# Two matmul groups moved ahead of a third, and a weight pass with another schedule, in a one-core decoder layer

## The chip, the cores and the metric

The kernel runs on one core of one Trainium2 chip. The metric is the device time of one execution in microseconds (us). Five engines take part, each with an instruction queue of its own that it works through in order: TensorE (PE, matmuls; its weight loads are PEld), VectorE (DVE), ScalarE (ACT), GpSimd (POOL) and SyncE (SP). SP and POOL also issue most transfers, each on a DMA queue of its own; both queues share 16 DMA engines. An instruction that waits for a semaphore holds up everything behind it on its engine.

## The reference

A decoder layer on x (2 x 512 tokens, 1024 features) is computed in float32, in three parts:

```
x = x + attn(layernorm(x))     # mamba2 block, then an MLP
x = x + fake_quant(layernorm(x)) @ fake_quant(ctx)
x = x + ffn(layernorm(x))
```

Two stages matter here. The MLP at the end of the first part is

```
mlp = silu(h2 @ gate_w.T) * (h2 @ up_w.T) @ down_w.T     # 1024 -> 3584 -> 1024
```

and the last part needs a mean over its own weights before it can begin:

```
def _binary_diff_weight(w, base):
    d = w - base
    coeff = jnp.mean(jnp.abs(d))
    return base + coeff * jnp.sign(d)     # for w1, w2 and w3
```

sign(d) and the sum of |d| depend on weights alone, so they can be computed at any time before the last part.

## The kernel before

**Order of the stages.** mamba2 takes the first 460 us or so, then the MLP's gates run to about 1110 us, its down product to about 1442, with the quantised product beside it and shortly behind, and from about 1446 us the gates and then the down product of the last part, which use the same functions.

**The gates** (`gates`) work in NG = 14 groups of 256 hidden columns. In a group, gate and up are each a product of a 1024 x 256 weight with the activations, split by a Strassen-Winograd scheme into seven products of blocks, 1 to 7. Products 1 and 2 go into one tile O12. In groups 0 and 1 they are plain matmuls: `first_two` makes four steps, each four matmuls into a PSUM bank (tile ma, line 355) and a copy to O12 by ScalarE (line 361). From group 2 they are a second level of the scheme (`second_level`, tiles mm2a to mm13d, lines 876 to 901). Products 6 and 7 are always a second level (tiles mn0a to mn13d). Products 5, 4 and 3 are plain (`one`, line 1027, tiles m0c, m0d); product 3 accumulates onto a bank of product 5 or 4 that DVE has read before (`onto`).

The order on TensorE is written out by hand and kept by chains (`on_pe`, `on_act`, `on_dve`): each instruction of a chain is issued after the one before it. In group 0 it is products 4 and 5, then mn0, then m0c onto m0c (product 3); then group 1 begins with ma. What closes a group, `finished`, `last_product` and `put` (the last sums, the product h3, the sums of mh and their store mhd), runs in the next group's beginning, through the list `late`.

**In `second_level`** four banks a, b, c, d are filled in the order a, b, c, d, b, a, c. The last matmul group adds onto c, and must wait until DVE has read c for the sum C22 (lines 199 and 202 are the helpers `add` and `sub` that make all these sums). `summed` runs between DVE's first sum (u2) and the second (u3): in mm it calls `last_product`, in mn `summed67`.

**The weight pass** (`Diffs`) is the side work in the MLP's gates: 34 steps, each for one weight group of the last part. A step subtracts the base from the weight (DVE, tile sw, 128 x 2048), takes Sign (ScalarE, line 1458, into the base's own tile, smean_w) and Abs with its sum (line 1459), stores the signs (POOL's queue, line 1460), and calls `load` for a later step (two transfers of 1 MB on POOL's queue, line 1449). POOL's transfers are kept in program order. Weight and base have two slots each (pool raw, tags raw and base). `gates` calls a step as `side` at three points of a group: in `summed67`, after the three products of `product`, and in `last_product`. In group order these are called C, A and B below: A ends group i, B stands in the mm and C in the mn of group i + 1.

After the gates, `down` reads the stored blocks back on SP's queue (line 1281) into places that include the pool raw's; in its first calls of `work` it also finds coeff from the sums (`find_coeff`, line 1498).

Of the kernel before, what the change touches and what calls it, by code (L numbers as in the profile page):

```python
# [10 lines left out]
F32 = mybir.dt.float32  # L11
# [6 lines left out]
P = 128  # L18
NB = 2
L = 512  # L20
D = 1024
KC = D // P
# [3 lines left out]
GW = 256  # L26
NG = INTER // GW
# [11 lines left out]
def decoder(ctx, tc, a, out):  # L39
# [266 lines left out]
    last = {}  # L306
# [9 lines left out]
    def on_act(fn):  # L316
        return ordered(act_last, fn)
# [10 lines left out]
    def last_on(engine):  # L328
        return next(ins for ins in reversed(traced) if ins.engine == engine)
# [11 lines left out]

        return {x: g.enter_context(tiles_waited(name=f"{name}{x}", bufs=counts.get(x, POOLS[x]), **kw)) for x in names}

    def first_two(name, act, pl, i, gw, uw, banks):

        O = pl["o12" if "o12" in pl else "o1"].tile([P, 2, 2, L], F32, tag="o", name=f"{name}o12_{i}")
        ps = []

        def step(p, x, w):
            if not p:  # L350
                ps.append(bank(banks[x], f"{name}a{x}_{i}"))

            def product():
                for k in range(4):
                    nc.tensor.matmul(  # L355
                        ps[x], w[:, 4 * p + k, :P], act[0][:, 4 * p + k, :],
                        start=not p and k == 0, stop=k == 3, skip_group_check=p > 0,
                    )

            on_pe(product)  # L360
            on_act(lambda: nc.scalar.copy(O[:, p, x, :], ps[x]))  # L361

        return O, [lambda p=p, x=x, w=w: step(p, x, w) for p in range(2) for x, w in enumerate((gw, uw))]

# [61 lines left out]
    with ExitStack() as m:  # L426
# [10 lines left out]
        pl = {  # L437
            "p1": proj.enter_context(tiles_waited(name="wp1", bufs=2)),
            "tmp": proj.enter_context(tiles_waited(name="wtmp", bufs=3)),
        }  # L440
# [296 lines left out]
        o = m.enter_context(tiles_waited(name="wout", bufs=1))  # L737
# [129 lines left out]

    def second_level(name, banks, p1, A, B, O, copied=lambda: None, summed=lambda: None, early=False, between=lambda: None):


        ps = {x: bank(k, f"{name}{x}", (P, 2, Q)) for x, k in zip("abcd", banks)}

        def mm(x, i, onto=False):
            for q in range(2):
                for k in range(2):
                    nc.tensor.matmul(
                        ps[x][:, q, :], A[i][:, q, k, :], B[i][q][:, k, :] if isinstance(B[i], tuple) else B[i][:, q, k, :],
                        start=not onto and q == 0 and k == 0, stop=k == 1, skip_group_check=onto or q > 0,
                    )

        c11, u2, u3, c22 = (O[:, :, x, c : c + Q] for x in (0, 1) for c in (0, Q))
        on_pe(lambda: mm("a", 1))
        on_act(lambda: nc.scalar.copy(p1, ps["a"]))
        copied()
        on_pe(lambda: mm("b", 6))
        on_dve(lambda: add(u2, p1, ps["b"]))
        summed()
        on_pe(lambda: mm("c", 5))
        if early:
            on_pe(lambda: mm("a", 2, True))  # L890
            on_act(lambda: nc.scalar.copy(c11, ps["a"]))
            on_pe(lambda: mm("b", 7, True))
            on_pe(lambda: mm("d", 4))
        else:
            on_pe(lambda: mm("d", 4))
            on_pe(lambda: mm("b", 7, True))
        on_dve(lambda: add(u3, p1, ps["b"]))
        on_dve(lambda: add(c22, u3, ps["c"]))
        if not early:
            on_pe(lambda: mm("a", 2, True))  # L900
            on_act(lambda: nc.scalar.copy(c11, ps["a"]))
        between()
        on_dve(lambda: add(u3, u3, ps["d"]))
        on_pe(lambda: mm("c", 3, True))
        on_dve(lambda: add(u2, u2, ps["c"]))
# [3 lines left out]
    def gates(name, act, acts, g, pl, weights, down_weight, begun, ex, side, third=()):  # L909
# [14 lines left out]
        with g:  # L924
# [73 lines left out]
            coming = [weights(0, None), weights(1, None)]  # L998
            w2, stored = [down_weight(0, None)], None
            A, A67 = left(0, *coming[0])  # L1000
            for i in range(NG):
                last = i == NG - 1
# [37 lines left out]
                elif i < 2:  # L1040
                    O12, steps = first_two(name, act, pl, i, *coming[0], X)
# [22 lines left out]
                if i == 0:  # L1064
                    c, d = (one("c", 4), one("d", 5)) if third else (one("c", 5), one("d", 4))
                elif third and i == 1:
                    c = one("d", 4)
# [5 lines left out]
                O67 = pl["o67"].tile([P, 2, 2, L], F32, tag="o", name=f"{name}o67_{i}")  # L1073

                def summed67(i=i, O12=O12):
# [8 lines left out]
                    if third:  # L1084
# [3 lines left out]
                            A54 = third_left(i, *coming[0])  # L1088
                        on_act(lambda: nc.scalar.activation(O12[:, 1, 0], O12[:, 1, 0], AF.Silu))

                second_level(f"{name}n{i}", Y, p1, A67, B67, O67, summed=summed67)
                on_dve(lambda: add(O67[:, 0], O12[:, 0], O67[:, 0]))

# [5 lines left out]
                turn = on_dve(lambda: add(O67[:, 1], O67[:, 0], O67[:, 1]))  # L1099
                h = pl["hp"].tile([P, 7, L], F32, tag="h", name=f"{name}h{i}")  # L1100
                C12, C22, C21 = O67[:, 0], O12[:, 0], O67[:, 1]
                if more:
                    c = one("c", 3)
                elif third:
                    e = one("c" if i else "e", 3)
                    if i:
                        d = one("e", 5)
                else:
                    if i:
                        c = one("c", 5)  # L1110
                    onto(C22, C21, c)
                    if i:
                        d = one("d", 4)
                    blocks21 = onto(C21, C21, d)
                    one("c", 3, True)
                coming.pop(0)
                if not last:
                    with tc.issue_after(turn):
                        steps = [], []
# [5 lines left out]
                if i == 1:  # L1125
                    b = act[0].rearrange("p (q k) l -> p q k l", q=2)
# [37 lines left out]
                    onto(O67[:, 0], O67[:, 0], c, on_dve)  # L1164
                    on_act(lambda: nc.scalar.activation(O67[:, 0, 0], O67[:, 0, 0], AF.Silu))

                def last_product(O67=O67, h=h, last=last):
                    if not last:
                        side(on_dve)
                    on_dve(lambda: nc.vector.tensor_tensor(h[:, 3, :], O67[:, 0, 0], O67[:, 0, 1], ALU.mult))  # L1170

# [34 lines left out]
                if third and last:  # L1206

                    def last_stores(i=i, h=h):
                        nc.sync.dma_start(dram[0][i][:, 1:3, :], h[0][:, 1:3, :])
                        hidden_blocks(h[0])  # L1210
                        nc.sync.dma_start(dram[0][i][:, 3:, :], h[0][:, 3:, :])

                    hl = []
                    def first_slot(finished_third=finished_third, hl=hl, i=i):
                        nc.sync.dma_start(hl[0][:, 0, :], dram[0][i][:, 0, :])
                        finished_third()

                    rest.extend([first_slot, lambda hl=hl: last_products(h=hl[0]), lambda hl=hl: last_stores(h=hl), hl.append])
                elif third:
                    late.extend([finished_third, last_products, put])  # L1220
                else:
                    for slot, o in ((0, O12[:, 1]), (2, C22), (1, C21)):
                        product(slot, o)
                    if not last:
                        with tc.issue_after(blocks21):
                            side(lambda fn: fn())
                    late.extend([finished, last_product, put])
# [185 lines left out]
    pl = {**mpl, **open_pools(g, "m", ("raw",))}  # L1413
# [20 lines left out]
    class Diffs:  # L1434
# [16 lines left out]
        def step(self, dve):  # L1451
            if self.n == len(self.todo):
                return
            i, j = self.todo[self.n]
            w, b = self.raw.pop(self.n)
            dve(lambda: sub(w, w, b))
            sg = b.bitcast(BF16)[:, : KC * GW]
            on_act(lambda: nc.scalar.activation(sg, w, AF.Sign))  # L1458
            on_act(lambda: nc.scalar.activation(w, w, AF.Abs, accum_out=sums[:, j, 2 * i : 2 * i + 1]))  # L1459
            ordered(self.pool_last, lambda: nc.gpsimd.dma_start(signs[j][i], sg))  # L1460
            self.load(self.n + 2)
            self.n += 1

    diffs = Diffs()
# [28 lines left out]
    def find_coeff():  # L1493
        nc.vector.tensor_reduce(tot, sums, AX.X, ALU.add)
        ones = xp.tile([P, P], F32, name="ones")
        nc.gpsimd.memset(ones, 1.0)
        ps = psx.tile([P, 512], F32, tag="x", name="cps2")
        nc.tensor.matmul(ps[:, 0:3], ones, tot, start=True, stop=True)
        nc.vector.tensor_scalar(coeff, ps[:, 0:3], 1.0 / (INTER * D), None, ALU.mult)
# [102 lines left out]
    steps = [0]  # L1602

    def work():
        steps[0] += 1
        if steps[0] == 4:
            find_coeff()
        if steps[0] == 10:
            contexts[0].load()
        if steps[0] in (12, 13):  # L1610
            contexts[0].column(steps[0] - 12)
        for _ in range(2):
            if pending:
                pending.pop(0)()
# [6 lines left out]
    pl = open_pools(held, "f", ("o12", "o67"))  # L1621
# [42 lines left out]
    third = [more[:, k].rearrange("p (q b c) -> p q b c", q=2, b=2) for k in range(3)]  # L1664
# [81 lines left out]
```

## Time and profile before

| | us |
|---|---|
| time, median of 3 runs | 2394.27 |
| lowest and highest run | 2389.66 to 2397.71 |
| span of the profiled execution (its own time) | 2391.7 |
| TensorE busy in it | 2337.4 |
| VectorE busy | 1744.0 |
| ScalarE busy | 620.2 |
| weight pass, first and last subtraction start | 497.5 and 994.0 |
| TensorE busy from 500 to 550 us, of 50 | 41.21 |
| TensorE busy from 569 to 1036 us, of 467 | 465.30 |

The span runs from the first to the last instruction of one execution. Lines of the profile are read like this. A group line names the source line, engine and operation, the tile written and the tiles read (out<-in), and a count. In a listing in order of time the first two numbers are the start and the duration in us; what stands in brackets at the end is the time that the engine idled just before and what ended it. A line of waits reads "who <- for whom: us in total, times, longest". A line of transfers gives the issuing queue, the count, the KB of each and the us from issue to landing. A matmul of float32 is two records, so that x8 is a group of four.

### The profile page before, as it was taken

The page shows a single profiled execution, that of the slowest core. Times are in us where ns is not written, and L with a number is a line of the kernel's source. Part 1 is how long each engine was busy: PE and PEld are TensorE (multiplying, and loading weights), DVE is VectorE, ACT ScalarE, POOL GpSimd, SP SyncE. Part 2 cuts the span into 40 slices and gives each one's busy share as a digit, 9 for nine tenths or more (in the row PEclk, how much of TensorE's full clock was granted, in tenths as well). Part 3 has the DMA queues.
Part 4 walks back from the last instruction along what each step waited for, and adds up shares of the span by engine and source line. Part 5 has one row for each costly group of instructions (what it writes and reads, how often), then busy time and mean ns, then how long its engine had stood idle before and what let it go on. Part 6 is the DMA issues. An engine that isn't in the chain of part 4 may idle for free.

```text
span 2391.7 us, 24259 instructions
## 1 busy us (share of the span) xinstructions
PE 2337.4 (98%) x9020; PEld 1649.0 (69%) x9028; DVE 1744.0 (73%) x2537; ACT 620.2 (26%) x800; POOL 207.0 (9%) x246
## 2 busy tenths in 40 slices
PE   7999999989999999999999999999999999999999
PEld 5445444446667667667888784578787787888888
DVE  5658777577888888865655756798888888775554
ACT  3355460333243234200000325122232232100000
POOL 1124211101011011000000101000000000000000
PEclk9999999999999999999999999999999999999999
DMA  4353541668888888838755471667677576786651
GB/s 160 115 201 120 183 173 71 163 243 325 313 329 336 309 328 335 294 156 299 229 165 161 131 228 54 179 167 203 192 190 210 165 206 205 249 261 196 191 176 63
DMA packets 183925, 494.80 MB, mean 207 GB/s; under 512 B 21504, under 2 KB 125952, under 8 KB 152832
## 3 DMA queue, kind: packets, MB, share of 16 engines
q1 hardware_dynamic: 155648, 334.91, 40.2%
q0 software_dynamic: 23552, 149.96, 21.7%
q10 hardware_dynamic: 4608, 8.39, 0.9%
q8 instruction: 71, 1.16, 0.2%
q14 instruction: 46, 0.38, 0.1%
HBM read 349.52 MB, written 145.75 MB: 207 GB/s over the span
## 4 chain that ended last, share of the span: by engine, by line
PE 62%; DVE 23%; DMA 5%; issue 4%; ACT 3%; SPq 2%; POOL 1%; DVEq 0%; POOLq 0%; ACTq 0%
PE op L769 3%; DVE fo L199 2%; DVE sw L202 2%; SPq L1281 2%; DVE mpl L199 2%; DVE fy L202 2%; DVE mo L199 1%; DVE down L202 1%; DVE mpl L202 1%; ACT smean_w L1458 1%; DVE fw L199 1%; DVE acc L635 1%; PE fa L355 1%; DMA f1b<-fwd 1%; PE dps L503 1%
## 5 line engine op out<-in xcount | busy, mean ns | idle before, releaser
L1458 ACT ACTIVATE smean_w<-sw 128x2048 bf16<-128x2048 f32 x34 | 65.0, 1911 | 177.3 <-DVE sw L202 177.3
L1641 ACT ACTIVATE fw<-fpl,coeff 128x2048 f32<-128x2048 bf16 x38 | 75.9, 2000 | 33.0 <-PE f1e L1027 12.9
L1642 POOL DMA_DIRECT2D fw<-in_mean_w x42 | 36.5, 869 | 544.9 <-DVE fo L199 310.2
L202 DVE TENSOR_TENSOR sw<-sw,smean_w 128x2048 f32<-128x2048 f32 x34 | 77.6, 2284 | 3.7 <-DMA smean_w<-in_mean_w 3.7
L1459 ACT ACTIVATE sw<-sw 128x2048 f32<-128x2048 f32 x34 | 64.9, 1910 | 1.1
L199 DVE TENSOR_TENSOR fo<-fo,fo 128x1024 f32<-128x1024 f32 x50 | 61.2, 1225 | 3.8 <-ACT fw L1641 0.5
L414 POOL TENSOR_TENSOR raw<-raw,base 128x1024 f32<-128x1024 f32 x16 | 44.4, 2777 | 199.1 <-DMA base<-in_mean_w 55.9
L769 PE MATMUL op<-wout,mz 128*128 128x512 f32 x128 | 56.6, 592 | 0.0
L1460 POOL DMA_DIRECT2D sign<-smean_w x34 | 18.3, 538 | 295.4 <-ACT smean_w L1458 295.3
L769 PEld LDWEIGHTS op<-wout,mz 128*128 128x128 f32 x128 | 23.9, 190 | 27.7 <-issue 27.0
L1188 ACT ACTIVATE fo<-fo 128x512 f32<-128x512 f32 x42 | 26.2, 630 | 43.8 <-DVE fo L199 43.8
L202 DVE TENSOR_TENSOR down<-down 128x512 f32<-128x512 f32 x56 | 37.2, 682 | 0.1
L1159 ACT ACTIVATE mo<-mo 128x512 f32<-128x512 f32 x28 | 17.7, 632 | 68.9 <-DVE mo L199 68.8
L199 DVE TENSOR_TENSOR fw<-fw 128x512 f32<-128x512 f32 x52 | 34.5, 684 | 0.4
L199 DVE TENSOR_TENSOR hid<-hid,op 128x512 f32<-128x512 f32 x24 | 15.9, 683 | 24.2 <-PE op L769 24.2
L202 DVE TENSOR_TENSOR fy<-fw,fw 128x512 f32<-128x512 f32 x48 | 32.9, 686 | 0.4
L355 PE MATMUL fa<-x3T,fw 128*128 128x512 f32 x64 | 30.4, 624 | 2.1 <-ACT fo L361 2.1
L199 DVE TENSOR_TENSOR fo<-fo 128x1024 f32<-128x1024 f32 x26 | 31.8, 1221 | 0.5
L1159 ACT ACTIVATE mpl<-mpl 128x512 f32<-128x512 f32 x14 | 8.8, 630 | 89.0 <-DVE mpl L199 89.0
L202 DVE TENSOR_TENSOR mh<-mh 128x512 f32<-128x512 f32 x42 | 29.0, 689 | 0.9
L1449 POOL DMA_DIRECT2D smean_w<-in_mean_w x34 | 18.2, 534 | 126.6 <-DMA sign<-smean_w 50.4
L1560 PE MATMUL xa<-c,c1T 128*128 128x512 bf16 x122 | 28.1, 379 | 0.5 <-issue 0.2
(2514 smaller groups left out, 6011.2 us busy)
## 6 DMA issues: line engine op xcount, KB each, us to landing
fw<-in_mean_w POOLq DMA_DIRECT2D x42, 1024.0 KB, 11.5
sw<-in_w POOLq DMA_DIRECT2D x34, 1024.0 KB, 7.8
smean_w<-in_mean_w POOLq DMA_DIRECT2D x34, 1024.0 KB, 7.6
mwd<-down SPq DMA_DIRECT2D x14, 1792.0 KB, 5.7
mhd<-mh SPq DMA_DIRECT2D x13, 1792.0 KB, 10.3
fhd<-fh SPq DMA_DIRECT2D x13, 1792.0 KB, 8.1
fpl<-sign SPq DMA_DIRECT2D x38, 512.0 KB, 8.8
sign<-smean_w POOLq DMA_DIRECT2D x34, 512.0 KB, 6.0
```

What stands on the lines that cost most here:

```text
L199: return nc.vector.tensor_tensor(out_, x, y, ALU.add)
L202: return nc.vector.tensor_tensor(out_, x, y, ALU.subtract)
L355: nc.tensor.matmul(ps[x], w[:, 4 * p + k, :P], act[0][:, 4 * p + k, :], start=not p and k == 0, stop=k == 3, skip_group_check=p > 0,)
L414: sub_ = nc.gpsimd.tensor_tensor(w, w, self.base[n % 2], ALU.subtract).ins
L769: nc.tensor.matmul(ps, A[p][:, k, t * P : t * P + P], B[p][:, k, :], start=(k == 0), stop=(k == 3))
L1159: on_act(lambda: nc.scalar.activation(o[:, 0], o[:, 0], AF.Silu))
L1281: load = nc.sync.dma_start(tl[:, c, :], dr[c][:, slot, col * Q : col * Q + Q]).ins
L1458: on_act(lambda: nc.scalar.activation(sg, w, AF.Sign))
L1459: on_act(lambda: nc.scalar.activation(w, w, AF.Abs, accum_out=sums[:, j, 2 * i : 2 * i + 1]))
L1560: nc.tensor.matmul(ps, self.c1T[:, k, c : c + P], self.c2[k // 4][:, k % 4, hs], start=(k == 0), stop=(k == KC - 1))
L1641: on_act(lambda: nc.scalar.activation(dst, src, AF.Identity, scale=coeff[:, j : j + 1]))
L1642: nc.gpsimd.dma_start(dst, a[base][i].rearrange("p a b -> p (a b)"), accum_op=ALU.add)
```

## The change

Five things are edited.

- In group 0 of the MLP, `first_two` of group 1 is called before product 3 of group 0, with banks 0 and 1 and with an own place for its O12: a tile of the pool raw with the tag raw. `begun[1]` tells group 1 that its first two products exist.
- A step of the weight pass is called ahead of the second level of group 0; the calls in `product` and `last_product` are left out in groups 0 and 1. So groups 0 and 1 have three steps, group 2 has C and every later one A, B and C up to the end; the 34th step falls into group 12, not 11.
- `step` loads for the next step (n + 1), and the first step loads nothing. Before, step n loaded for n + 2.
- `find_coeff` runs in the sixth call of `work`, not the fourth, and after the last DVE instruction issued by then.
- `second_level` of group 1 and what closes group 0 follow from `begun`: with group 1 in it, `finished` and `last_product` of group 0 are called at once, and `put` in `summed67`.

```diff
-    def first_two(name, act, pl, i, gw, uw, banks):
-        O = pl["o12" if "o12" in pl else "o1"].tile([P, 2, 2, L], F32, tag="o", name=f"{name}o12_{i}")
+    def first_two(name, act, pl, i, gw, uw, banks, O=None):
+        if O is None:
+            O = pl["o12" if "o12" in pl else "o1"].tile([P, 2, 2, L], F32, tag="o", name=f"{name}o12_{i}")
...
+                if not third and not i:
+                    side(on_dve)
                 second_level(f"{name}n{i}", Y, p1, A67, B67, O67, summed=summed67)
...
+                if not third and i == 0:
+                    place = pl["raw"].tile([P, KC * GW], F32, tag="raw", name=f"{name}o12_1")
+                    place = place.rearrange("p (a b c) -> p a b c", a=2, b=2)
+                    begun[1], steps = first_two(name, act, pl, 1, *coming[1], (0, 1), place)
+                    for step in steps:
+                        step()
...
-                def last_product(O67=O67, h=h, last=last):
-                    if not last:
+                def last_product(O67=O67, h=h, last=last, i=i):
+                    if 1 < i < NG - 1:
                         side(on_dve)
...
-                    if not last:
+                    if 1 < i < NG - 1:
                         with tc.issue_after(blocks21):
                             side(lambda fn: fn())
...
-            self.load(self.n + 2)
+            if self.n:
+                self.load(self.n + 1)
             self.n += 1
...
-        if steps[0] == 4:
-            find_coeff()
+        if steps[0] == 6:
+            with tc.issue_after(last_on(mybir.EngineType.DVE)):
+                find_coeff()
```

## The prediction

> **What bounds the kernel now.** I read the page's busy shares first, then TensorE's waits in the stretch that the diff touches, then that stretch in order of time, and last one later group of the same loop, engine by engine.
>
> ```profile
> PE 2337.4 (98%) x9020; PEld 1649.0 (69%) x9028; DVE 1744.0 (73%) x2537; ACT 620.2 (26%) x800; POOL 207.0 (9%) x246
> ```
>
> TensorE (PE) is busy for 98% of a span of 2391.7 us. An edit that only reorders work can win no more than PE's gaps in its stretch, and it loses whatever new gap it opens. PE's waits from 440 to 640 us (us in total, times, longest):
>
> ```profile
> PE m0c L1027 <- DVE mo L199: 4.6, 1, 4.6
> PE ma L355 <- ACT mo L361: 3.0, 1, 3.0
> PE mn1c L876 <- DVE mpl L199: 1.2, 1, 1.2
> PE mm2c L876 <- DVE mo L199: 0.4, 1, 0.4
> ```
>
> The first is group 0's third product (m0c onto m0c), the second is group 1's first product (ma). PE in order of time there:
>
> ```profile
> 503.53 1.93 PE L876 MATMUL mn0c<-mt,mpl 128*128 128x256 f32 x8
> 510.03 5.40 PE L1027 MATMUL m0c<-h2T,mg0s 128*128 128x512 f32 x8 [4.57 <-DVE mo L199]
> 515.26 3.60 PE L1027 MATMUL m0c<-h2T,mu0s 128*128 128x512 f32 x8
> 528.71 3.70 PE L355 MATMUL ma<-h2T,gate_w 128*128 128x512 f32 x8 [2.98 <-ACT mo L361]
> ```
>
> The same eight matmuls take 5.40 us after the wait of 4.57 us and 3.60 after none: a wait of that length costs a further 1.8 us at a slower clock. After the wait of 2.98 us it is 0.1.
>
> **Part 1, group 1's first two products go ahead of group 0's third (gain 9.8 us).** No matmul is added or removed. The built order has the four ma groups between mn0c and m0c. From start to start a group of eight takes 3.44 us, and mn0c 1.73, so the new PE order is: ma from 505.3 to 519.0, m0c to 525.9, then mn1a, which stands at 535.68 now. Is each ready? ma writes banks 0 and 1. Bank 1 was read by DVE at 502.0 and bank 0 by ScalarE's copy, done at 504.3. The third product waits for DVE's adds at 509.3 to 511.8, which are long over at 519. ScalarE's copies of ma come before Silu in its new order, so the 2.98 us wait behind the two weight-pass activations goes too. What is late next is mn1a: it needs group 1's sums, done at 520.2, and bank 4, which the add of m0c frees at about 524.3, as DVE's three products wait for Silu, and Silu for the table load (1.28 us) that now follows the last copy at 519.7. That is 1.6 us of cover; if it failed, PE would wait by the excess alone. mn1c's wait of 1.2 us stays: four sums of mh, one of mg1s and a weight-pass subtraction (2.28 us) stand between mn1b's adds. Gain 535.7 - 525.9 = 9.8, and the wait at mm2c goes with the two steps taken from ahead of it: 0.6 by start to start. Together 10.4.
>
> The new place is a slot of raw whose last reader is ScalarE's Abs of step 1, at 503.6; the first copy into it comes at 508.7. Nothing waits. Step 0 moves to about 484.4 on DVE, where its loads have landed (469.38 + 11.9); it pushes second-level sums by 2.3 us, to 490, and PE reads them at 494.9.
>
> **Part 2, the weight pass loads one step ahead instead of two (cost).** This is what decides. A step is a subtraction on DVE (sw), Sign and Abs on ScalarE, a store of the sign and two loads of 1 MB on POOL's queue. Step n used to load for n+2; now it loads for n+1, behind its own sign store, and all three are issued in order. Steps come in threes, at A, B and C:
>
> ```profile
> 613.81 2.28 DVE L202 TENSOR_TENSOR sw<-sw,smean_w 128x2048 f32<-128x2048 f32 x1
> ...
> 621.18 2.29 DVE L202 TENSOR_TENSOR sw<-sw,smean_w 128x2048 f32<-128x2048 f32 x1
> ...
> 625.30 0.69 DVE L199 TENSOR_TENSOR mo<-mo,mm3c 128x512 f32<-128x512 f32 x1
> ...
> 632.20 2.28 DVE L202 TENSOR_TENSOR sw<-sw,smean_w 128x2048 f32<-128x2048 f32 x1
> ...
> 636.71 0.69 DVE L199 TENSOR_TENSOR mpl<-mpl,mn3b 128x512 f32<-128x512 f32 x1 [1.08 <-PE mn3b L876]
> ```
>
> ```profile
> 618.44 0.54 POOL L1460 DMA_DIRECT2D sign<-smean_w  x1 [17.03 <-ACT smean_w L1458]
> 620.47 0.53 POOL L1449 DMA_DIRECT2D sw<-in_w  x1 [1.50 <-ACT sw L1459]
> 622.67 0.53 POOL L1449 DMA_DIRECT2D smean_w<-in_mean_w  x1 [1.67 <-DMA sign<-smean_w]
> ```
>
> B comes 7.4 us after A, C 11.0 after B, the next A 26.8 after C. DVE's order from group 3 to group 11 is unchanged in the built kernel, so these positions stay. With A as zero: the sign store is issued at 4.63 (it waits for Sign), the loads for B right behind it, the second at 5.7, since their slots have long been free. When do they land? The issues of the two loads above, each asked for alone, KB and us to landing:
>
> ```profile
> sw<-in_w POOLq DMA_DIRECT2D x1, 1024.0 KB, 6.7
> ```
>
> ```profile
> smean_w<-in_mean_w POOLq DMA_DIRECT2D x1, 1024.0 KB, 7.3
> ```
>
> So smean landed at 8.86 + 7.3 = 16.2. An earlier issue helps little: from the sign's landing to the end of a window of 613 to 632 us nearly every slice shows the DMA engines at 9 tenths or more, with the down read (1 MB, issued at 5.2) between. The trace has no such trio issued back to back, so bounds: at least 3.4 us for the sign (issue at 548.41) and twice 2.75 for the loads (the nearest two such landings, 544.87 and 547.62), that is 4.63 + 8.9 = 13.5; at most 17.7, the latest of today's (577.45 + 8.8, A at 568.59). I take 16.2, the nearest row.
>
> DVE is in order: behind B's subtraction stand the product L1170, one sum, and the adds of mm3b and mm3c, and PE's mm3c waits for the latter's bank, with all of mn3 behind it. It waits for it today: 4.86 us after B (621.18 to 626.04), PE free only 0.3 earlier. So B's lateness, 16.2 + 0.1 - 7.4 = 8.9 us (6.2 to 10.4), goes to PE whole, and 1.8 us of slow clock follows, as at m0c.
>
> C: seen from B, the loads meet the store mhd only from 10.4 on. I take a landing at 14.4 (13.5 to 17). C would stand at 11.0 + 1.8 = 12.8, so it is 1.6 late; 1.2 of it are cover (DVE's idle 1.08 before 636.71 and 0.1 on PE): 0.4 us (0 to 3.0). The next A has 26.8 us and waits for nothing. A triple costs 8.9 + 1.8 + 0.4 = 11.1 us (8.0 to 15.2).
>
> How many: 34 steps; three in groups 0 and 1, one C in group 2, then thirty in ten triples, A in groups 2 to 11. 10 x 11.1 = 111 us (80 to 152).
>
> The Trainium skill, page "DMA: Bandwidth & Descriptors", section "Anatomy of one DMA", gives about 2.0 us plus bytes at 436 GB/s: estimated, the trio would land 8 us after the sign's issue, at 12.6, B would be 5.3 late and the whole change +61 us. Its section "Queues, rings and completion order" says that each engine takes queues in turn, so that the down read costs the loads a share, which brings the estimate to 15.0; the measured 16.2 is later than either, and I go by it.
>
> **Part 3, the end of the pass moves from group 11 to group 12 (nothing).** SP's reads for the down stage wait for the last step's places. They start at 993.8 now and would at about 1047 plus the delay; 26 issues take some 17 us and PE needs the first at 1112. Cover: about 45 us; without it SP's later weight traffic would be late by the excess. find_coeff moves to step 6 of the work calls: its matmul (0.28 us) and reduction stand beside mo6c, where DVE idles 1.42 us; 0 to 0.3 us.
>
> **Sum.** +111 - 10.4 = +101 us on the execution's 2391.7: 2492. Against the median of 2394.27 that is 2495.
>
> **Rivals.**
> *The gain alone: 2384 us.* The loads land in time and 10.4 us is all. For it: DMA bytes per group are unchanged. Against it: A's loads are issued at 5.7 and B comes at 7.4, while the quickest load of 1 MB near took 5.0 us. It decides below 1.0 us per triple (10.4 / 10), so from a landing at 8.4 instead of 16.2. Chance 0.05.
> *Half of each: no change.* The wait is hidden by PE's queue. Against it: PE waits at mm3c already. 0.02.
> *Light queues: 2405 to 2460.* Longer groups thin the DMA traffic, landing before 13.5. 0.05.
> *A worse queue: over 2540.* SP's transfers go first wherever both queues hold work, and C waits as long as B. Above 152 us. 0.08.
> The forecast case, 2460 to 2540, has 0.80.
>
> **Numbers.** Predicted 2495; range 2460 to 2540 from the bounds 2391.7 + 80 - 10.4 and + 152 - 10.4, shifted by 2.6 and rounded. A measurement here tells 0.3% (7 us) from no change. Faster 0.05, within 0.3% 0.02, slower 0.05 + 0.80 + 0.08 = 0.93.
>
> **What would show it.** Right: DVE's subtractions wait for the DMA smean_w some 20 times, ten of 8 to 9 us; PE waits ten times at mm3c to mm12c for DVE mo, with the matmuls behind slower; mn1a stands near 526 and the waits at m0c and ma are gone; the group's period grows from 45.2 to some 56 us. Wrong: B at 7.4 us after A, or sign stores and loads in another order on POOL, or PE at mm3c without a wait while DVE has one.

## The result and the profile after

The changed kernel takes 2495.13 us (median; 2491.93 to 2501.12) against 2394.81 us (2389.66 to 2397.71) of the kernel before beside it: ratio 1.0431, 95% interval 1.0413 to 1.0449, so it is slower by 100 us. The profiled execution of after is the slowest of its runs (own time 2501.12, span 2499.1 us), 107.4 us over the span of before; part of these 107.4 comes before the change begins, as shown below.

The line of busy times on the page of after:

```profile
PE 2361.0 (94%) x9020; PEld 1666.2 (67%) x9028; DVE 1744.3 (70%) x2537; ACT 620.0 (25%) x800; POOL 205.3 (8%) x246
```

The counts of instructions are those of before, on every engine. TensorE has 23.6 us more of busy time for the same 9020 records (matmuls at a slower clock), and the rest of the longer span is waiting. Its waits from 440 to 1230 us (who <- for whom: us in total, times, longest):

```profile
PE mm5c L877 <- DVE mo L199: 9.3, 1, 9.3
PE mm12c L877 <- DVE mo L199: 9.3, 1, 9.3
...
PE mm4c L877 <- DVE mo L199: 8.6, 1, 8.6
PE mn12c L877 <- DVE mpl L199: 3.3, 1, 3.3
...
PE mn1c L877 <- DVE mpl L199: 0.8, 1, 0.8
PE mn4c L877 <- DVE mpl L199: 0.6, 1, 0.6
```

The waits at m0c and ma are gone. In their place stand ten waits, one in the mm of each group from 3 to 12, 8.6 to 9.3 us each and 88.5 us in all. They are waits for DVE's sums mo, but these sums are not the cause: they stand behind the weight pass's subtraction on DVE, and the first line of DVE's own waits in the same stretch is

```profile
DVE sw L202 <- DMA smean_w<-in_mean_w: 99.2, 18, 9.1
```

that is, the weight pass's subtraction waits for its second load, and PE stands behind DVE. One triple of steps shows the chain, first DVE's subtractions and then POOL's queue in order of time (start, duration; in brackets the idle time before and what ended it):

```profile
607.21 2.28 DVE L202 TENSOR_TENSOR sw<-sw,smean_w 128x2048 f32<-128x2048 f32 x1
...
623.03 2.29 DVE L202 TENSOR_TENSOR sw<-sw,smean_w 128x2048 f32<-128x2048 f32 x1 [8.37 <-DMA smean_w<-in_mean_w]
...
637.41 2.29 DVE L202 TENSOR_TENSOR sw<-sw,smean_w 128x2048 f32<-128x2048 f32 x1 [0.93 <-DMA smean_w<-in_mean_w]
```

```profile
611.84 0.54 POOL L1469 DMA_DIRECT2D sign<-smean_w  x1 [25.19 <-ACT smean_w L1467]
612.39 0.53 POOL L1458 DMA_DIRECT2D sw<-in_w  x1
613.01 0.53 POOL L1458 DMA_DIRECT2D smean_w<-in_mean_w  x1
```

Step A begins at 607.21. Its store of the sign is issued 4.63 us later, when Sign has ended, and the two loads for step B right behind it without a wait of their own. The means land at 622.94, 15.7 us after A, and B starts at 623.03 where it would be ready to start 8.4 us sooner. PE in the same stretch:

```profile
617.41 1.89 PE L877 MATMUL mm3a<-h2T,gate_w 128*128 128x256 f32 x8
627.90 3.78 PE L877 MATMUL mm3c<-h2T,mpl 128*128 128x256 f32 x8 [8.60 <-DVE mo L199]
631.48 2.48 PE L877 MATMUL mn3a<-mt,mg3s 128*128 128x256 f32 x8
633.79 1.89 PE L877 MATMUL mn3b<-mpl,mpl 128*128 128x256 f32 x8
```

After the wait of 8.60 us the next four matmuls (eight records) take 3.78 us in place of 1.89, and the four after them 2.48. The granted clock in these two stretches is 0.50 (627.90 to 631.48 us) and 0.74 (631.48 to 633.79). By the starts that is a further 2.4 us here; behind the ten waits it is 1.7 to 3.1 us, 2.2 on average.

Where the time goes, by the starts of the stages in both traces (my readings, after minus before, us):

```
first gates group, mn0a   +4.2     (h2T, far ahead of the edits: +4.4)
mn1a                      -5.5
mm3a                      -6.6
mm4a                      +4.2
mm8a                     +48.0
mm12a                    +92.3
mm13a                   +108.5
mo1a, f0c, fn1a   +108.5, +108.6, +108.2
end                     +107.4
```

From mn0a to mm3a the changed kernel wins 10.8 us; from mm3a to mm13a it loses 115.1 us, about 11 in each of ten groups (their period grows from 45.2 to about 56 us); afterwards little changes any more (1.1 us by the end). The first +4.2 arises before the stretch that the edits reach and is no part of the change: the same stage, h2T, starts between 436.4 and 445.1 us in the nine executions profiled here, in code that is the same in all.

### The profile page after: what moved, and what is told of

Same layout as the page of the kernel before. It is cut to its first block, busy times and chain, and to the rows that moved or that the text cites. A ratio compares the mean times of both kernels' runs of the same rounds, so it can differ in the third digit from the quotient of the medians.

```text
span 2499.1 us, 24260 instructions
## 1 busy us (share of the span) xinstructions
PE 2361.0 (94%) x9020; PEld 1666.2 (67%) x9028; DVE 1744.3 (70%) x2537; ACT 620.0 (25%) x800; POOL 205.3 (8%) x246
## 4 chain that ended last, share of the span: by engine, by line
PE 38%; DVE 10%; DMA 3%; SPq 3%; issue 1%; ACT 1%; POOL 0%; DVEq 0%; POOLq 0%; ACTq 0%
SPq L1290 2%; DVE fo L199 2%; DVE fy L202 2%; DVE fw L199 1%; PE fa L356 1%; PE xa L1570 1%; PE m12c L1028 1%; PE mo6c L1301 0%; PE mo4c L1301 0%; PE fo7a L1301 0%; PE fo4c L1301 0%; PE fo3c L1301 0%; PE fo5c L1301 0%; PE fo2c L1301 0%; PE mo3c L1301 0%
## 5 line engine op out<-in xcount | busy, mean ns | idle before, releaser
L202 DVE TENSOR_TENSOR fh<-fh 128x512 f32<-128x512 f32 x39 | 26.9, 689 | 0.9
```

Source lines behind the costliest of these rows:

```text
L202: return nc.vector.tensor_tensor(out_, x, y, ALU.subtract)
```

## The experiments

The theory (D in the expectations): the time between the issue of a load and its subtraction decides, and nothing else in the change costs. Rivals: the slots in which the new schedule puts its steps, or the pool's places (S); loads that are slow at any distance because the DMA engines are full (Q). All times are medians, with the ratio to the kernel before on the same chip.

### Loads two ahead again, the rest of the change kept

```diff
-            if self.n:
-                self.load(self.n + 1)
+            for n in {0: (), 1: (2,), 2: (3, 4)}.get(self.n, (self.n + 2,)):
+                self.load(n)
```

> The changed kernel with only the loads of the weight pass put back to two steps ahead (step 1 loads for 2, step 2 for 3 and 4, later steps for n + 2). Theory D (the price is the distance in time between a load and its subtraction): nothing is left but the gain of the new order, 10.4 us, so 2384 us (2381 to 2390), PE without a wait at mm3c to mm12c, DVE waiting less than 10 us for smean_w. Rival S (the price is the slot of the pool raw that group 1's products occupy, or the new schedule of steps): still 2480 or more, since place and schedule stay. Rival Q (the loads are slow at any distance because they share the DMA engines): 2440 or more.

Measured: 2384.22 us, ratio 0.9958 (0.9941 to 0.9974). From mn0a to mm3a it wins 10.8 us, as after does, and then keeps all but 0.4 of it. PE's waits in the gates are down to these:

```profile
PE mn1c L877 <- DVE mpl L199: 0.8, 1, 0.8
PE mm12c L877 <- DVE mo L199: 0.2, 1, 0.2
```

So the moved products, the new place and the new slots of the steps cost nothing measurable; the one line on the loads costs all of it, 111 us (2495 - 2384).

### The kernel before, with only the loads one step ahead

```diff
-            self.load(self.n + 2)
+            if self.n:
+                self.load(self.n + 1)
```

> The kernel before with one edit: a step loads for n + 1 instead of n + 2 (the first step for none). Order, places and schedule of steps are the old ones. Theory D: eleven triples instead of ten, each some 11 us as in the changed kernel, the first at 12 to 13 as its B stands only 3.4 us behind A: 2394 + 125 = 2519 us (2505 to 2530), and PE waits of 8 to 10 us in every group from 2 on. Rival S: no place is taken from the pool and the schedule is the old one, so 2394 to 2400.

Measured: 2521.73 us, ratio 1.0542 (1.0518 to 1.0565). PE's two longest waits in the gates and the shortest of the long ones:

```profile
PE mm5c L876 <- DVE mo L199: 9.6, 1, 9.6
PE mm2c L876 <- DVE mo L199: 9.5, 1, 9.5
...
PE mn1c L876 <- DVE mpl L199: 8.0, 1, 8.0
```

The same waits arise without any other part of the change, eleven in place of ten, since the old schedule has its triples of steps from the first groups on. With the first experiment this settles that the one line is enough for the loss, and that there is no loss without it.

### Loads one step ahead, but issued in front of the step's own store

```diff
-            ordered(self.pool_last, lambda: nc.gpsimd.dma_start(signs[j][i], sg))
             if self.n:
                 self.load(self.n + 1)
+            ordered(self.pool_last, lambda: nc.gpsimd.dma_start(signs[j][i], sg))
```

> The changed kernel, still loading one step ahead by count, but each step issues its loads on POOL's queue before its own sign store instead of behind it, so that they need not wait for this step's subtraction and Sign. Theory D: the loads for B then go out some 9 us after the C before, not 5 us after A, and land ahead of B; C's land at about A + 17 of 18.4; 2384 us (2380 to 2394) as with two steps ahead. Rival S: unchanged, 2480 or more. Rival Q: 2440 or more.

Measured: 2382.33 us, ratio 0.9956 (0.994 to 0.9972), the same as with the loads two ahead; no wait of PE in the gates is over 0.8 us. POOL's queue in this version shows why:

```profile
611.80 0.54 POOL L1471 DMA_DIRECT2D sign<-smean_w  x1 [2.60 <-ACT smean_w L1467]
613.83 0.55 POOL L1458 DMA_DIRECT2D sw<-in_w  x1 [1.50 <-ACT sw L1468]
617.73 0.53 POOL L1458 DMA_DIRECT2D smean_w<-in_mean_w  x1 [3.35 <-DVE mh L202]
622.82 0.54 POOL L1471 DMA_DIRECT2D sign<-smean_w  x1 [4.56 <-ACT smean_w L1467]
```

Behind a store come loads that wait for that step's own Abs (1.50 us): they fill the slot that this step frees, and so belong to the step after next. In the queue, load n + 1 in front of store n stands right behind store n - 1, which is where "two ahead" puts it: apart from the first steps, the order is that of the first experiment. In after the loads behind the store wait for nothing, because their slots had stood empty for a whole step. So "one or two ahead" in the code is, on this queue, a question of on which side of a waiting store the load stands.

### Step B called later (behind `turn`, after mn's part), loads as in after

```diff
                 turn = on_dve(lambda: add(O67[:, 1], O67[:, 0], O67[:, 1]))
+                if not third and 1 < i < NG - 1:
+                    side(on_dve)
...
                 def last_product(O67=O67, h=h, last=last, i=i):
-                    if 1 < i < NG - 1:
-                        side(on_dve)
```

> The changed kernel, still one step ahead and behind the sign store, but B's step is called after the group's last sum of product 7 (turn) instead of in last_product. The distances become A to C 18.4, C to B about 11, B to A some 16 to 20 us. Theory D: only B is late, by 3 to 4 us, and it stands ahead of sums for which PE has some 6 us in hand, so 2384 to 2400 us, and no PE wait over 2 us at mm3c to mm12c. Rival S and rival Q: as many bytes, slots and steps as in the changed kernel, so 2470 or more.

Measured: 2466.25 us, ratio 1.0318 (1.0292 to 1.0344), a miss: only 29 us of the 111 come back. DVE still waits 54.2 us for the means, and PE waits in another place:

```profile
PE mm10b L877 <- DVE mo L199: 8.9, 1, 8.9
...
PE mm11b L877 <- DVE mo L199: 4.4, 1, 4.4
```

The moved step itself waits by at most 1.2 us now (the one at 650.52 not at all, its means landed at 650.1). But it now comes shortly before A, and its trio for A, issued at 655.15 to 656.32, meets the reads of gate_w (654.61) and up_w (658.04) on SP's queue. The means take 13.3 us and land at 669.62; A waits 4.28 us for them. And A has no cover: behind its Sign and Abs, which are in order on ScalarE, stands the copy for the second level's first sum, and behind that PE's mm4b:

```profile
677.23 3.57 PE L877 MATMUL mm4b<-mex,mpl 128*128 128x256 f32 x8 [5.45 <-DVE mo L199]
```

What was wrong in my expectation: it gave A a gap of 16 to 20 us in place of 26.8 and still took B alone to be late. Without its wait A would stand 14.9 us behind B, and its means landed 19.1 us behind B. The move made the gap ahead of B larger by taking from the gap ahead of the next A, and a load for a step in a small gap was late there too.

### The same, with the loads in front of the store

The edit is the last two together.

> The version with step B called later (behind turn), with each step's load issued ahead of its own store of the sign. Theory (only the time from a load's issue to its use matters; a load that goes ahead of the store is issued a step's length earlier and is in time in any slot): no wait of VectorE for the means, time 2380 to 2392. Rival (the slot of step B behind turn costs by itself, through what stands behind it on ScalarE): 2440 or more, with the waits of TensorE at mm3b to mm12b still there and VectorE not waiting for the means.

Measured: 2394.23 us, ratio 1.0008 (0.9997 to 1.002); the upper end of what D expected is passed by 2 us, and the rival's 2440 is far off. DVE does not wait for the means in the gates at all, so the lateness of the loads was the cause in the fourth experiment too. What remains is the rival's share, and it is small: each of ten groups has

```profile
PE mm4b L877 <- DVE mo L199: 1.1, 1, 1.1
```

and a period of 46.2 us against 45.2 in the third experiment. In it DVE has no idle time for 20 us before step A (from 633.5 to 653.8); with the moved step's 2.28 us in the same stretch, A starts 0.6 us after mm4a, where in the third experiment it starts 1.6 before it, and ScalarE's copy for mm4b stands behind A's Sign and Abs. So the less lucky slot costs 1 us a group, some 10 us in all (2394 - 2382 = 12); the short lead of the loads costs 113.

### The new steps alone

After, with group 1's first two products behind group 0's third again (no `begun[1]`, no place of its own) and the loads two ahead:

```diff
-                if not third and i == 0:
-                    place = pl["raw"].tile([P, KC * GW], F32, tag="raw", name=f"{name}o12_1")
...
-            if self.n:
-                self.load(self.n + 1)
+            self.load(self.n + 2)
```

> The new schedule of the weight pass alone: first_two and the place of its own are out, group 1's first two products stand again behind group 0's third, and every load is issued two steps ahead. Theory (order and steps are separate gains, 10.8 us together): the wait at m0c stays with 4.6 us and the 1.8 us of slow clock behind it, the waits at ma and mm2c go, because their steps now come in other slots; time 2389 to 2392 against 2394, and the order's own share is the 6 to 7 us that are left to the version with the order and loads two ahead (2384). Rival (the new slots of the steps are what takes all the waits away, the order adds nothing): 2383 to 2385 and no wait at m0c. Rival (the new slots cost something that the order hides): over 2396.

Measured: 2390.03 us, ratio 0.9982 (0.9971 to 0.9993). PE still waits at m0c, and the matmuls behind take 6.41 us instead of 3.60:

```profile
513.97 6.41 PE L1028 MATMUL m0c<-h2T,mg0s 128*128 128x512 f32 x8 [4.57 <-DVE mo L199]
```

From mn0a to mm3a this version wins 4.4 us and the first experiment 10.8. So the new slots of the steps bring 4.4: the waits at ma (3.0), mn1c (1.2) and mm2c (0.4) are gone, with the small losses behind them 5.4 in all, and the matmuls behind m0c's wait took 1.0 more this time. The order of the products brings the other 6.5: m0c's wait and the slow matmuls behind it, less 0.8 that PE waits at mn1c again. The medians give 2390.0 - 2384.2 = 5.8. A version with the order alone would need a place for the early O12 outside the pool raw, or the old steps beside it in raw; it wasn't tried.

### After, without the reads of the down weights beside the trio

```diff
-        t8 = pl["t8"].tile([P, 8, 512], F32, tag="t8", name=f"down{i}")
-        nc.sync.dma_start(t8[:, :4, :], a["down_w"][i])
+        if not i:
+            kept8.append(pl["t8"].tile([P, 8, 512], F32, tag="t8", name=f"down{i}"))
+            nc.sync.dma_start(kept8[0][:, :4, :], a["down_w"][i])
+        t8 = kept8[0]
```

> The changed kernel, loads one step ahead, with the down weights of group 0 used for all groups, so the later groups' down weights are not read (that part of the computation is changed). Theory that the read that runs beside the three transfers sets their landing: the means land some 13.6 us after step A in place of 15.7 to 16.5, step B is late by 6.2 us and PE waits some 6 in place of 8.6 to 9.3 in each of ten triples; time about 2469 (2455 to 2478). Rival (the three transfers in their queue take their time whatever runs beside them): landing stays at 15.7, time 2490 to 2500.

Measured: 2481.38 us, ratio 1.0375 (1.0358 to 1.0393): between the two theories. Over the ten triples the means for B land 13.7 to 14.6 us after A (mean 14.2), against 15.7 to 16.5 (mean 16.0) in after. PE's longest and shortest wait:

```profile
PE mm8c L877 <- DVE mo L199: 7.5, 1, 7.5
...
PE mm7c L877 <- DVE mo L199: 6.5, 1, 6.5
```

The read beside costs 1.8 us a triple, and the stretch from mm3a to mm13a is longer than before by 96.3 us instead of 115.1. That is a sixth of the loss. The rest is there with nothing beside the trio: 4.6 us from A to the issue of the store, and then, in the triple shown next, 9.8 us until 2.5 MB of store and loads have gone through. The DMA engines are the limit in most of them. The stretch of the trio without the read (busy times, then the granted clock, the DMA engines' busy share and GB/s):

```profile
607.00:610.00 3.00, 3.00 (x16) 2.64 (x15) 0.69 (x1) 1.08 (x3) 0.15 (x1) 1.00 0.99 295
610.00:613.00 3.00, 2.91 (x14) 2.22 (x12) 0.00 (x0) 0.00 (x0) 0.00 (x0) 1.00 0.95 396
```

The store was issued at 605.45; from 607 to 613 us the engines are 95 to 99% busy, with no other transfer issued. In the 1.6 us before and the 2.3 us behind they are 30 and 38% busy: a start and an end that are paid as well. So Q is right about the size: a trio that begins with the store took about 10 us even with nothing beside it. It is not the cause by itself, since the same transfers cost nothing where they begin earlier.

How the read beside costs its 1.8 us can be seen in after, in the transfers of the stretch from 614.8 to 617.3 us (packets, MB and share of the 16 engines by queue; q1 is SP's, q0 POOL's):

```profile
q1 hardware_dynamic: 127, 1.04, 98.9%
q0 software_dynamic: 16, 0.00, 0.3%
```

SP's read was issued 0.04 us behind sw's load and goes through whole, while POOL's loads stand. In nine of the ten triples it is so: the read is issued within 0.06 us of sw's load, and in the same 2.5 us of the triple its queue has 94 to 99% of the engines' time. In the remaining one, that of 719.38, it is issued 0.75 us behind sw's load, and in these 2.5 us the two queues have 38 and 41%; the means land 16.5 us after A there, no sooner than in the others. What decides between the two is not shown.

## Why the prediction was right

**The gain of the order: 10.4 predicted, 10.8 measured.** ma starts 1.8 us after mn0c as thought, m0c and ma have no wait, and mn1a moves by 9.8 us (to 530.13, of which 4.2 are the drift before the stage: 525.9, the number predicted). The wait at mn1c stayed, at 0.8 us. The new place held nothing up. The split of the gain was partly wrong: the working put the end of ma's wait down to the new order of ScalarE's copies, and the version with the new steps alone shows that the steps' new slots are enough for it. So 6.5 come from the order and 4.4 from the steps.

**The landing of B's loads: A + 16.2 predicted, 15.7 to 16.5 measured**, B late by 8.9 predicted, PE's wait 8.6 to 9.3. The choice between bounds 13.5 and 17.7 was the nearest row, a load of 7.3 us issued at A + 8.9. In the event the means' load, issued at A + 5.8, took 9.9 us: an earlier issue bought next to nothing, as the text said. The reason given for it, engines that are full with the down read between, holds by the last experiment only in part. The read of the down weights costs 1.8 us, and most of the landing time is the trio's own. That the row of a load issued 3 us later, behind other transfers, gave the landing within 0.5 us is therefore in part luck; the bounds were worked out, and the landing lay inside them. The Trainium skill's rule of about 2.0 us plus bytes at 436 GB/s (page "DMA: Bandwidth & Descriptors", section "Anatomy of one DMA") gave an estimate of 8 us from the store's issue; in the two triples shown 9.8 were measured with no read beside it and 11.1 with the read, so the measured row was the better guide. Taken once for three transfers, the formula has one start of 2 us and then the full rate; in the trace without the read the 3 us from 607 to 610, in which the store ends and the loads begin, move 295 GB/s, and the next three 396. Its section "Queues, rings and completion order" says that each engine takes the queues it has work for in turn, and the estimate made from it put the read's share at 2.4 us (15.0 - 12.6). 1.8 were measured, and in nine of the ten triples the read went through whole; whether POOL's loads had work queued on the engines by then, no row shows.

**The slow clock: 1.8 predicted for each wait, about 2.2 measured.** The 115.1 us of the ten triples less 88.5 of waits at mm and 4.3 at mn leave 22.3, and by the starts of the matmuls the ten waits are followed by 22.0 us of lost time. This is the term of the sum that was mis-sized, and it explains most of 115 against 111. The 1.8 came from a single wait, and the length of a wait does not fix the price: the same 4.57 us at m0c was followed by 1.8 us in before, 2.8 with the new steps alone and 2.4 in before with the loads one ahead, and four waits of 8.60 us in after by 1.7 to 3.1. What fixes it is not shown.

**C: B + 14.4 predicted, 13.5 to 14.7 measured** in the first nine triples, with a wait of PE of at most 0.6 us, as said (0.4). In the last triple, in group 12, it is 17.3 after B, and PE waits 3.3 us at mn12c, just outside the bounds given (17, 3.0). In that triple the store took 4.8 us to land, sw's load 8.5 and the means' 11.5, where the trio for C in the triple shown above has 2.9, 6.6 and 8.5, with no other transfer issued between 1126 and 1141.67. In the version without the down reads the same triple is the latest too (C starts at B + 16.0, the others at 13.8 to 15.7). Why is open; it is worth 5 us.

**The end of the pass: nothing predicted, nothing measured.** The shift is +108.5 us at mm13a, at mo1a and, within 0.1, at f0c. The 45 us of cover for SP's reads were enough.

**The sum** of +101 us came to +100 by the medians and +107 by the profiled executions, and the 4.2 us before the stage are part of the difference between these two. Of the rivals, the gain alone (2384) exists, but as a different kernel: it is what the first and third experiments measure, 0.9958 (0.9941 to 0.9974) and 0.9956 (0.994 to 0.9972), and both beat the two kernels of this case. Light queues failed on the trio's own time, which has 84% of the loss even with the read gone (96.3 of 115.1). A worse queue had its mechanism right, since SP's read does go first in nine of ten triples; its price is 1.8 us a triple, and C does not wait as long as B.

## What to carry to other kernels

Count a prefetch in microseconds from where its issue really stands in its queue, not in steps of the loop: behind a store that waits for the step's own result, the lead is what is left after that result, and with steps 7 us apart it was less than the transfers needed. Where a queue issues in order, put the loads that can go at once in front of the store that must wait; one line here is worth 113 us. When a step is moved to give one load more room, look at the room that it takes from the next one, and at what stands behind that next step on every engine.

## What the runs showed of the hardware

- A store of 512 KB and two loads of 1 MB, issued within 1.2 us on one queue with nothing beside them, took 9.8 us until the last had landed (version without the down reads, triple of 600.82). A read of 1 MB on the other queue, issued some 0.6 us after the store, had the engines almost alone for 2.5 us in nine of ten triples, and lengthened the trio by 1.8 us on average over ten.
- The matmuls behind a wait of TensorE were slower only where the wait was long, and the price did not follow its length. In after, waits of 8.6 to 9.3 us were followed by 1.7 to 3.1 us of lost time (granted clock 0.50 in the first 3.6 us at mm3c), a wait of 3.26 us at mn12c by 1.6 (granted clock 0.53). After 4.57 us it was 1.8 in before and 2.8 with the new steps alone; after 2.98 us in before 0.1 (granted clock 1.00).
- Nine profiled executions reached the same point (h2T) between 436.4 and 445.1 us, in code that no edit touches. Compared from mn0a to mm3a instead, the six that have the moved products win 10.8 us each over before. A difference of spans alone would have put 4 us of drift down to the change.
